# Mixture-of-experts layers: the third block of rows transposed whole, and the transposes of the next expert split in two pairs

## The chip, the cores and the metric

The kernel runs on one core of a Trainium2 chip. The metric is the time that one execution takes on the device, in microseconds (us), as the median of several runs.

## The reference, cut to what matters

The input x has 8 x 1024 rows of 512 float32 numbers. Three layers follow each other: a mixture-of-experts layer, an attention layer with 16 heads, and the same mixture-of-experts layer again. Each works on the layer-normed x and is added to x, the experts' layers with a factor of 0.5. The change lies in the experts' layers alone:

```python
xt = x.reshape(T, H)                       # T = 8192 rows, H = 512
logits = xt @ w_router                     # E = 32 experts
top1 = argmax(softmax(logits)); gate = probs[top1]
pos = position of the row among those of its expert
accepted = pos < C                         # C = 320 = 1.25 * T / E
buf[e, pos] = xt                           # (E, C, H), the accepted rows by expert
g = einsum("ech,ehf->ecf", buf, w_gate)
u = einsum("ech,ehf->ecf", buf, w_up)
y = einsum("ecf,efh->ech", silu(g) * u, w_down)
out = xt + where(accepted, y[slot] * gate, 0)
```

Everything is float32.

## The kernel before

**Experts one after another.** After routing, `experts` sorts the 32 experts by how many rows they got and takes one of several compiled profiles of widths. In the profiled execution the widths are 320 for the first 10 experts in either layer, then 288 for 9, 256 for 8 and 224 for 5. A width of over 256 means three blocks of up to 128 rows (`NB` = 3; the third block has 64 rows of an expert's capacity of 320), a width of up to 256 means two. `gather` fetches the rows of an expert two experts ahead, by indirect DMAs of POOL's queue. `load` orders the three weight matrices wg, wu and wd of the next expert on SP's queue; they have two buffers each, so each load waits until the last matmul that read the buffer is done.

**One expert.** `feed(now, following, after)` runs one expert (`now`) and prepares the next (`following`). The engines PE, ACT, DVE and POOL work in the order that the code writes down; nothing is reordered. Its steps:

1. DVE takes the statistics of the following expert's rows (`measure`).
2. For each of four parts f of the hidden width, `gated` (line 705) multiplies the transposed rows bT with wg and wu into the PSUM tiles gp and up; ACT takes the silu of gp into sg, and DVE multiplies sg and up into a (line 729). After f = 0 ACT normalizes the following rows into b (line 172), after f = 1 DVE prepares their residuals (line 186).
3. `put_others` (line 646, 650) scales and writes two blocks of other rows, those that pass an expert layer by.
4. `transpose` (lines 685 to 696) turns the following expert's b, four column blocks k of 128, each over all its blocks of rows, into a PSUM tile of tag tp (two buffers), which DVE copies to bT (line 696).
5. The down products: for each block i of rows PE sums four products with wd into yp (line 744; line 752 for the third block, which is laid out as 2 x 64 rows of 256), DVE scales yp by the gate and adds the residual into ys (line 748, 758), and POOL writes ys to its rows by an indirect DMA (line 762).

A float32 matmul on 512 columns appears in the trace as two records, so a block of down products has eight, while a transpose has one.

**The transposes before the change.** In `transpose` a block of the expert that has fewer than 128 rows within the capacity of 320 is turned at its own size:

```python
for i, at in enumerate(range(0, C, P)):
    m = min(P, C - at)
    nc.tensor.transpose(
        tp[:, at : at + m], to.b[:m, i, k * P : (k + 1) * P], s.ident[:m, :m]
    )
```

So the third block is a transpose of 64 rows (in the trace "64*128" for its weight load, with b as the weights, and 64 moving columns of the identity). `begin` does the same once per layer for the first expert, with four PSUM tiles at once (line 608).

PSUM has two buffers for each of the tags tp, gp, up and yp.

Of the kernel before, what the change touches and what calls it, by code (L numbers as in the profile page):

```python
# [13 lines left out]
F32 = mybir.dt.float32  # L14
# [8 lines left out]
P = 128  # L23
# [12 lines left out]
def at_once(steps):  # L36

    while True:
        try:
            next(steps)  # L40
        except StopIteration as end:
            return end.value
# [503 lines left out]
class Expert:  # L546
# [34 lines left out]
    def begin(self, to):  # L581

        nc, s, ap = self.nc, self.s, self.ap
        to.mv = ap.tile([P, to.NB, 2], F32, tag="mv", name="mv")
        to.by = [
            ap.tile([P, to.NB], F32, tag=name, name=name) for name in ("rstd", "nmr", "r2", "n2")
        ]
        to.b = ap.tile([P, s.NB, s.D], F32, tag="b", name="b")
        to.bT = ap.tile([P, s.KD, s.C], F32, tag="bT", name="bT")
        steps = []  # L590
        for i in range(to.NB):
            at = slice(i, i + 1)
            s.stats(ap, to.mv[:, i, :], to.x[:, i, :])
            steps.append(s.normalizing(ap, to.mv[:, at, :], [t[:, at] for t in to.by]))
            next(steps[i])
            if i:
                at_once(steps[i - 1])
        at_once(steps[-1])
        assert s.KD == 4
        tps = [  # L600
            self.ps.tile([P, s.C], F32, tag=tag, name="tp") for tag in ("tp", "up", "tp", "up")
        ]
        C = min(to.NB * P, s.C)
        for i in range(to.NB):
            s.normalize(to.b[:, i, :], to.x[:, i, :], to.by, i)
            m = min(P, C - i * P)
            for k, tp in enumerate(tps):
                nc.tensor.transpose(
                    tp[:, i * P : i * P + m], to.b[:m, i, k * P : (k + 1) * P],
                    s.ident[:m, :m],  # L610
                )
        for k, tp in enumerate(tps):
            (nc.scalar.copy if k % 2 else nc.vector.tensor_copy)(to.bT[:, k, 0:C], tp[:, 0:C])  # L613
        self.rests(to)
# [67 lines left out]
                    s.NB - 1, p,  # L682
                )

    def transpose(self, to):
        nc, s = self.nc, self.s
        C = min(to.NB * P, s.C)
        to.bT = self.ap.tile([P, s.KD, s.C], F32, tag="bT", name="bT")
        for k in range(s.KD):
            tp = self.ps.tile([P, C], F32, tag="tp", name="tp")  # L690
            for i, at in enumerate(range(0, C, P)):
                m = min(P, C - at)
                nc.tensor.transpose(  # L693
                    tp[:, at : at + m], to.b[:m, i, k * P : (k + 1) * P], s.ident[:m, :m]
                )
            nc.vector.tensor_copy(to.bT[:, k, 0:C], tp)

    def gated(self, to, f):
        nc, s, width = self.nc, self.s, to.width
# [13 lines left out]
    def feed(self, now, following, after):  # L713

        nc, s = self.nc, self.s
        n, half, KF = s.last, s.D // 2, s.KF
        a, wd = s.acts[now.r % 2], now.weights[2]
        others = self.fetch_others(now.r) if self.others else None  # L720
        if following:
            self.measure(following)
        later = after and after()
        for f in range(KF):
            sg, up = self.gated(now, f)
            if following and f == 0:
                self.scales(following)
                self.normalize(following)
            nc.vector.tensor_tensor(a[:, f, 0 : now.width], sg, up, ALU.mult)  # L729
            if following and f == 1:  # L730
                self.rests(following)
        if others:
            self.put_others(now.r, others)
        if following:
            self.transpose(following)
        for i in range(now.NB):
            yp = self.ps.tile([P, s.D], F32, tag="yp", name="yp")
            ys = self.ap.tile([P, s.D], F32, tag="ys", bufs=3, name="ys")
            gate = self.gates[:, i * s.E + now.r : i * s.E + now.r + 1]
            index = self.go[:, i * s.E + now.r : i * s.E + now.r + 1]  # L740
            to = self.views[now.r * s.NB + i]
            if i < s.NB - 1:
                for f in range(KF):
                    nc.tensor.matmul(  # L744
                        yp, a[:, f, i * P : (i + 1) * P], wd[:, f, :],
                        start=(f == 0), stop=(f == KF - 1),
                    )
                nc.vector.scalar_tensor_tensor(ys, yp, gate, now.x[:, i, :], ALU.mult, ALU.add)  # L748
            else:
                for f in range(KF):  # L750
                    for c in range(2):
                        nc.tensor.matmul(  # L752
                            yp[c * n : (c + 1) * n, 0:half], a[:, f, i * P : s.C],
                            wd[:, f, c * half : (c + 1) * half],
                            start=(f == 0), stop=(f == KF - 1),
                        )
                ys = ys[:, 0:half]
                nc.vector.scalar_tensor_tensor(
                    ys, yp[:, 0:half], gate, now.rest, ALU.mult, ALU.add
                )  # L760
                to = to.rearrange("t (c d) -> (t c) d", c=2)
            nc.gpsimd.indirect_dma_start(
                out=to, out_offset=bass.IndirectOffsetOnAxis(ap=index, axis=0),
                in_=ys, in_offset=None, bounds_check=to.shape[0] - 1, oob_is_err=False,
            )
        return later


class Attention:
# [95 lines left out]
    def stage(self, top, sum_, fill, begin, whole=False):  # L865

        for i in range(self.SLOTS):  # L870
            self.now += 1
            prs = {}
            first, second = self.phases(top, sum_)
            self.phase(i, *first, prs)
            for rank, task in begin.get(i, ()):
                self.start(task, rank)
            self.step(1.3 if top else 4)
            if self.half:
                assert i not in fill
                self.group()  # L880
            elif i in fill:
                self.half = fill[i]()
                self.group()
                if whole:
                    self.group()
            if second:
                self.phase(i, *second, prs)
            self.last_sums()
            if sum_:
                self.behind.append((*sum_, i, prs))  # L890
            if not self.half:
                self.product()
            self.step(0.9)
# [603 lines left out]
```

## Time and profile before

| what | us |
|---|---|
| median of 3 runs | 4915.01 |
| lowest and highest | 4911.32, 4916.07 |
| the profiled execution | 4901.53 |
| its span in the profile | 4899.7 |
| PE (TensorE) busy in it | 4644.6 |
| transposes at line 693 | 640, of them 144 with 64 rows |

The profile is of one execution. Its page gives the busy time by engine, the chain of work that ended last and the costliest groups of instructions; "PE" is a matmul, "PEld" the load of its weights, which can overlap matmuls before it. A row of a group reads: line, engine, operation, out<-in by the tiles' names, shapes, count, then busy us, mean ns of one, and the idle time of the engine before it with what ended that idle time. A row of the timeline reads: start us, us, engine, line, operation, and the count of merged instructions. The expert stages run from about 172 to 989 us and from about 4078 us to the end of the span.

### The profile page before, as it was taken

How to read it: one execution, taken by the hardware profiler on the slowest of the kernel's cores; microseconds unless marked ns; L12 is line 12 of the kernel's file. 1: busy time of each engine (PE TensorE's matmuls, PEld its weight loads, DVE VectorE, ACT ScalarE, POOL GpSimd, SP SyncE). 2: the span in 40 equal slices, each digit the busy share in tenths (PEclk: the TensorE clock that was granted, in tenths of full speed). 3: DMA queues.
4: the chain of work that ended last, by engine and by line, in shares of the span. 5: the costliest groups of instructions: out<-in, count | busy, mean ns of one | idle time of the engine just before them, and what ended most of it. 6: DMA issues, size and time to landing. Idle time of an engine off the chain costs nothing.

```text
span 4899.7 us, 68858 instructions
## 1 busy us (share of the span) xinstructions
PE 4644.6 (95%) x24572; PEld 2131.3 (43%) x24572; DVE 2848.9 (58%) x5568; ACT 2924.6 (60%) x5856; POOL 790.6 (16%) x787
## 2 busy tenths in 40 slices
PE   6799999968899999999999999999999877999998
PEld 4466667722233333333333333333333224666676
DVE  8433333346666767767767767777777733333332
ACT  6211111118998888888888888888888831111111
POOL 4423332210000010110110100100001002222221
PEclk8899999979999999999999999999999988999999
DMA  4455556531112212212212212212211124445554
GB/s 140 164 169 184 183 192 204 183 92 29 32 31 59 74 38 64 69 42 65 69 41 68 72 38 67 70 40 66 63 46 54 51 68 166 161 155 174 165 183 135
DMA packets 290580, 486.01 MB, mean 99 GB/s; under 512 B 47895, under 2 KB 83169, under 8 KB 290224
## 3 DMA queue, kind: packets, MB, share of 16 engines
q1 hardware_dynamic: 255376, 404.36, 26.4%
q0 software_dynamic: 34560, 76.93, 5.1%
q8 instruction: 196, 3.21, 0.3%
q14 instruction: 160, 1.31, 0.1%
q10 hardware_dynamic: 288, 0.20, 0.0%
HBM read 380.11 MB, written 89.72 MB: 96 GB/s over the span
## 4 chain that ended last, share of the span: by engine, by line
PE 82%; DVE 8%; ACT 4%; issue 3%; DMA 2%; POOL 1%; SPq 1%; DVEq 0%; POOLq 0%; ACTq 0%
PE sa L1219 13%; PE gp L705 10%; PE up L705 9%; PE pq L1124 9%; PE po L1301 9%; PE yp L744 9%; PE sb L1199 6%; PE px L1327 4%; PE pv L1169 4%; PE sb L1226 3%; ACT junk L1238 2%; DVE nm L1234 2%; PE tp L693 2%; PE tp L194 1%; PE yp L752 1%
## 5 line engine op out<-in xcount | busy, mean ns | idle before, releaser
L1234 DVE TENSOR_REDUCE nm<-sa 128x2 f32<-128x1024 f32 x1024 | 1249.3, 1221 | 648.8 <-PE sa L1219 386.5
L1238 ACT ACTIVATE junk<-sa,nm 128x512 f32<-128x512 f32 x2048 | 1408.2, 688 | 257.7 <-DVE nm L1234 178.6
L1219 PE MATMUL sa<-k,q 32*128 32x512 f32 x4096 | 1149.0, 644 | 17.9 <-ACT junk L1238 11.2
L1231 ACT ACTIVATE pr<-sb 128x1024 f32<-128x1024 f32 x1024 | 1041.3, 1018 | 99.4 <-PE sb L1226 95.9
L1226 PE MATMUL sb<-q,k 32*128 32x512 f32 x4096 | 1062.0, 602 | 0.0
L710 ACT ACTIVATE sg<-gp 128x320 f32<-128x320 f32 (+3 forms) x256 | 102.8, 402 | 1231.6 <-PE gp L705 1081.8
L1149 POOL TENSOR_TENSOR raw<-raw,a 128x512 f32<-128x512 f32 x128 | 164.4, 1284 | 2401.3 <-DMA rot<-raw 1694.1
L1301 PE MATMUL po<-pr,v 128*32 128x512 f32 x4096 | 548.0, 606 | 0.1
L705 PE MATMUL gp<-bT,wg 128*128 128x320 f32 (+3 forms) x2048 | 532.4, 403 | 0.5 <-DVE bT L613 0.5
L705 PE MATMUL up<-bT,wu 128*128 128x320 f32 (+3 forms) x2048 | 525.0, 399 | 0.0
L1124 PE MATMUL pq<-hT,wqk 128*128 128x512 f32 x1024 | 512.2, 624 | 5.4 <-DVE raw L1139 4.4
L744 PE MATMUL yp<-wd,a 128*128 128x512 f32 x1024 | 453.7, 596 | 0.0
L705 PEld LDWEIGHTS gp<-bT,wg 128*128 128x128 f32 x2048 | 387.5, 191 | 116.4 <-issue 28.1
L1199 PE MATMUL sb<-mrow,ones 3*128 3x512 bf16 x2048 | 392.7, 384 | 41.8 <-ACT pr L1231 40.5
L705 PEld LDWEIGHTS up<-bT,wu 128*128 128x128 f32 x2048 | 389.2, 190 | 94.4 <-issue 0.4
L729 DVE TENSOR_TENSOR a<-sg,up 128x320 f32<-128x320 f32 (+3 forms) x256 | 114.1, 446 | 543.3 <-PE up L705 512.8
L1199 PEld LDWEIGHTS <-ones 3*128 3x128 bf16 x2048 | 99.7, 91 | 708.6 <-issue 670.7
L1238 ACT ACTIVATION_READ_ACCUMULATOR junk<-sa,nm 128x1 f32 x2048 | 398.1, 194 | 0.0
L1226 PEld LDWEIGHTS sb<-q,k 32*128 32x128 f32 x4096 | 359.5, 184 | 0.1
L1219 PEld LDWEIGHTS sa<-k,q 32*128 32x128 f32 x4096 | 304.8, 183 | 81.5 <-ACT pr L1231 30.1
L1124 PEld LDWEIGHTS pq<-hT,wqk 128*128 128x128 f32 x1024 | 176.5, 191 | 324.8 <-issue 228.0
L748 DVE SCALAR_TENSOR_TENSOR ys<-yp,gates,x 128x512 f32<-128x512 f32 x128 | 96.2, 751 | 368.9 <-PE yp L744 368.9
(178 smaller groups left out, 4277.3 us busy)
## 6 DMA issues: line engine op xcount, KB each, us to landing
wg<-in_w_gate SPq DMA_DIRECT2D x64, 1024.0 KB
wu<-in_w_up SPq DMA_DIRECT2D x64, 1024.0 KB
wd<-in_w_down SPq DMA_DIRECT2D x64, 1024.0 KB
rot<-raw SPq DMA_DIRECT2D x1024, 32.0 KB
all<-in_x SPq DMA_DIRECT2D x32, 512.0 KB
xt<-first_rows SPq DMA_DIRECT2D x64, 256.0 KB
xr<-first_rows SPq DMA_DIRECT2D x64, 256.0 KB
d<-inverse SPq DMA_DIRECT2D x256, 64.0 KB
```

What stands on the lines that cost most here:

```text
L705: nc.tensor.matmul(acc, w[:, k, f * P : (f + 1) * P], to.bT[:, k, 0:width], start=(k == 0), stop=(k == s.KD - 1),)
L744: nc.tensor.matmul(yp, a[:, f, i * P : (i + 1) * P], wd[:, f, :], start=(f == 0), stop=(f == KF - 1),)
L1124: nc.tensor.matmul(acc, w[:, which, k, :], self.hT[b, n][:, k, :], start=(k == 0), stop=(k == KD - 1),)
L1169: nc.tensor.matmul(acc, hT[:, k, at : at + P], self.w_vo[:, k, :], start=(k == 0), stop=(k == KD - 1),)
L1199: nc.tensor.matmul(sb[:, h, :], self.ones16[at : at + 3, :], row[at : at + 3, :], start=True, stop=False,)
L1219: nc.tensor.matmul(sa[:, h, :], qa[at, (g * 4 + j) * P : (g * 4 + j + 1) * P], ka[at, m * 512 : (m + 1) * 512], start=True, stop=True,)
L1226: nc.tensor.matmul(sb[:, h, :], k[at, t * P : (t + 1) * P], q[at, n * 512 : (n + 1) * 512], start=False, stop=True,)
L1231: nc.scalar.activation(pr, sb, AF.Exp)
L1234: nc.vector.tensor_reduce(nm[:, m, j, pair : pair + 2], sa, AX.X, ALU.max, negate=True)
L1238: nc.scalar.activation(self.junk, sa[:, h - pair, :], AF.Exp, bias=nm[:, m, j, h : h + 1], accum_out=se[:, m, j, h : h + 1],)
L1301: nc.tensor.matmul(self.po[at : at + HD, :], self.v[b][t][:, c * P + at : c * P + at + HD], prs[h // 2 * 2][:, h % 2, :], start=(t == 0), ...
L1327: nc.tensor.matmul(acc, self.oT[b, c, half][:, j * P : (j + 1) * P], self.w_vo[:, c, :], start=False, stop=(c == KD - 1),)
```

## The change

The third block is transposed at its full 128 rows and 128 columns, in `begin` and in `transpose`; the PSUM tiles tp are made 384 columns wide for three blocks, and only the first 320 columns are copied on, as before. The rows behind the 64 used ones are in b anyway, since gathering and normalizing treat 128 rows of each block.

`transpose` now takes the column blocks that it is to do. The first two (k = 0, 1) stand ahead of the first block's down products, the other two (k = 2, 3) ahead of the second block's. On DVE the copies of the second pair thereby stand behind the first block's ys. The order and the DMAs of ACT, POOL and SP stay as they were.

Of the semaphores that PE waits for, these move: the third and the fourth down product of a block wait for DVE's a of f = 2 and f = 3, and the first gp products of the next expert at k = 2 and k = 3 wait for DVE's copies.

```diff
@@ begin
         tps = [
-            self.ps.tile([P, s.C], F32, tag=tag, name="tp") for tag in ("tp", "up", "tp", "up")
+            self.ps.tile([P, s.NB * P], F32, tag=tag, name="tp") for tag in ("tp", "up", "tp", "up")
         ]
         C = min(to.NB * P, s.C)
         for i in range(to.NB):
             s.normalize(to.b[:, i, :], to.x[:, i, :], to.by, i)
-            m = min(P, C - i * P)
             for k, tp in enumerate(tps):
                 nc.tensor.transpose(
-                    tp[:, i * P : i * P + m], to.b[:m, i, k * P : (k + 1) * P],
-                    s.ident[:m, :m],
+                    tp[:, i * P : (i + 1) * P], to.b[:, i, k * P : (k + 1) * P], s.ident
                 )
@@ transpose
-    def transpose(self, to):
+    def transpose(self, to, ks):
         nc, s = self.nc, self.s
         C = min(to.NB * P, s.C)
-        to.bT = self.ap.tile([P, s.KD, s.C], F32, tag="bT", name="bT")
-        for k in range(s.KD):
-            tp = self.ps.tile([P, C], F32, tag="tp", name="tp")
-            for i, at in enumerate(range(0, C, P)):
-                m = min(P, C - at)
+        if 0 in ks:
+            to.bT = self.ap.tile([P, s.KD, s.C], F32, tag="bT", name="bT")
+        for k in ks:
+            tp = self.ps.tile([P, to.NB * P], F32, tag="tp", name="tp")
+            for i in range(to.NB):
                 nc.tensor.transpose(
-                    tp[:, at : at + m], to.b[:m, i, k * P : (k + 1) * P], s.ident[:m, :m]
+                    tp[:, i * P : (i + 1) * P], to.b[:, i, k * P : (k + 1) * P], s.ident
                 )
-            nc.vector.tensor_copy(to.bT[:, k, 0:C], tp)
+            nc.vector.tensor_copy(to.bT[:, k, 0:C], tp[:, 0:C])
@@ feed
         if others:
             self.put_others(now.r, others)
-        if following:
-            self.transpose(following)
         for i in range(now.NB):
+            if following and i < 2:
+                self.transpose(following, range(i * s.KD // 2, (i + 1) * s.KD // 2))
             yp = self.ps.tile([P, s.D], F32, tag="yp", name="yp")
```

## Prediction

> **What bounds the kernel now.** I read the page first, then the busy time by stretch of an expert stage, then the groups of line 693 (the transposes that the change touches), and last the order of time around single transposes. The page says who carries the span:
>
> ```profile
> span 4899.7 us, 68858 instructions
> PE 4644.6 (95%) x24572; PEld 2131.3 (43%) x24572; DVE 2848.9 (58%) x5568; ACT 2924.6 (60%) x5856; POOL 790.6 (16%) x787
> PE 82%; DVE 8%; ACT 4%; issue 3%; DMA 2%; POOL 1%; SPq 1%; DVEq 0%; POOLq 0%; ACTq 0%
> ```
>
> PE (TensorE) is busy 95% of the span and holds 82% of the chain that ended last. The expert stages, asked by stretch (columns: stretch, length, then busy time and count of PE, weight loads, DVE, ACT, POOL; granted clock; DMA share; GB/s), are tighter still:
>
> ```profile
> 450.00:690.00 240.00, 239.75 (x964) 155.87 (x963) 88.83 (x220) 45.81 (x80) 76.99 (x79) 1.00 0.57 186
> 690.00:960.00 270.00, 263.85 (x1101) 197.16 (x1100) 91.72 (x246) 54.32 (x99) 80.46 (x85) 1.00 0.62 206
> ```
>
> PE is busy for 239.75 of 240 us with DVE at 37% and DMA at 57%, clock at 1.00. So whatever PE time is removed here shortens the stage, unless something with slack becomes late. But busy is not the same as full: matmuls overlap, and a badly spaced one is still counted busy. The groups of the transposes (busy us, mean ns | idle before), for the first expert stage, show this:
>
> ```profile
> L693 PE MATMUL tp<-ident,b 128*128 128x128 f32 x248 | 48.3, 290 | 6.9 <-DVE bT L696 6.2
> L693 PE MATMUL tp<-ident,b 64*128 64x64 f32 x72 | 19.7, 274 | 0.0
> ```
>
> The small transposes (64 rows) occupy 19.7/72 = 0.274 us each, their whole duration: nothing overlaps them. The whole ones take 48.3/248 = 0.195. Now one phase of each kind, PE only, then the weight loads of the first:
>
> ```profile
> 640.78 0.41 PE L705 MATMUL up<-bT,wu 128*128 128x288 f32 x1
> 641.02 2.40 PE L693 MATMUL tp<-ident,b 128*128 128x128 f32 x12
> 643.35 0.70 PE L744 MATMUL yp<-wd,a 128*128 128x512 f32 x1
> ```
>
> ```profile
> 641.33 0.40 PEld L693 LDWEIGHTS tp<-ident,b 64*128 64x128 f32 x3 [0.17 <-issue]
> 641.90 0.14 PEld L693 LDWEIGHTS tp<-ident,b 64*128 64x128 f32 x1 [0.17 <-issue]
> 642.20 0.20 PEld L693 LDWEIGHTS tp<-ident,b 128*128 128x128 f32 x2 [0.16 <-DVE bT L696]
> ```
>
> ```profile
> 741.22 0.59 PE L705 MATMUL up<-bT,wu 128*128 128x256 f32 x2
> 741.65 0.60 PE L693 MATMUL tp<-ident,b 128*128 128x128 f32 x4
> 742.74 0.77 PE L693 MATMUL tp<-ident,b 128*128 128x128 f32 x4 [0.48 <-DVE bT L696]
> 743.34 1.02 PE L744 MATMUL yp<-wd,a 128*128 128x512 f32 x2
> ```
>
> The phase with three blocks lasts 643.35 - 641.02 = 2.33 us for 12 transposes. The one with two blocks lasts 743.34 - 741.65 = 1.69 us for 8, of which four come in a row: 0.60 us from first start to last end, less one duration of 0.273, over three steps: 0.109 us apart. That is the cadence without hindrance. The starts of the single records give the rest. With three blocks they lie 0.109, 0.203, 0.203, 0.165, 0.203 and so on apart: 0.20 into and out of every 64-row transpose, 0.165 for the next after it, since its weight load is no longer ahead (the 0.17 us idle before the 64-row loads). And once a phase there is a wait for DVE: with two PSUM buffers of tag tp, the third transpose tile waits until DVE has copied out the first; with three blocks that step takes 0.30 to 0.33 us, with two blocks 0.72 to 0.79, followed by three steps of 0.165.
>
> **The change part by part.**
>
> *How much there is to win.* The trace's groups have 640 transposes at L693, 144 of 64 rows: 144/4 = 36 phases of three blocks, and (640 - 432)/8 = 26 of two. From start of a phase to the first yp, the trace has 20 phases of 2.360 us (expert at work 320 wide), 16 of 2.328 (288), 2 of 1.721, 16 of 1.686 (256), 8 of 1.654 (224): 128.1 us in all.
>
> *What it becomes.* The count of transposes stays, all are 128x128, and no 64-row load is left, so each step is 0.109 us, the step into yp too (743.23 to 743.34). 36 x 12 x 0.1093 + 26 x 8 x 0.1093 = 70.0 us. Saved: **58.1 us**: 33.1 from whole third blocks (36 phases; 2.345 mean less 0.113 of stall less 1.312), 25.0 from the stall (36 x 0.113 + 26 x 0.805).
>
> *A rule that speaks against the first edit.* Row: 64-row transposes cost 0.203 us a step, whole ones 0.109. The Trainium skill, "TensorE: Matmul & The Clock Gate", section "Back-to-back issue gap", lists the gap by free size: 134 cycles for 128 columns, about 60 up to 64, so widening 64 to 128 more than doubles it. By that rule (estimate from 0.109) a small transpose should take 0.049 and the edit would lose 144 x 0.060 = 8.6 us. The trace decides, as its 0.203 was measured in this very stream. The tiling page of the skill ("TensorEngine Tiling (Array Packing)", "Key Properties") names what fits: a change of tiling mode drains the engine. That it is the change of 64 to 128 rows, not the change of PSUM tile, is seen in the two-block phase, whose four in a row go from the first tile to the second at 0.109.
>
> *Transposes in two pairs.* The third and fourth tile now come after the first block's down products (8 records of yp 0.429 us apart, 3.43 us). DVE copies the first two tiles right after the product for a at f=3: in the phase at 641.02 that product ends at +0.73, two copies at 0.48 follow by +1.75. PE comes back for tile three at 0.65 + 3.43 = +4.09: the wait is gone with 2.3 us to spare. The semaphore itself stays on the loads of tiles three and four, already satisfied; the trace has no satisfied DVE wait there. Ends: 0, as for the satisfied wait for wd at the first yp (0.109 after the last transpose), and 0.056 (0.165 less 0.109) for each, 62 x 2 x 0.056 = 7 us; a gain is excluded, 0.109 being the floor. I take 0, the nearer row. A new wait: yp for f=2 and f=3 now waits for DVE's a, which the transposes used to cover. f=2 comes at +0.65 + 4 x 0.429 = +2.37 (two blocks: +2.15), a is ready at +0.73: cost nothing, cover 1.4 us; without it, up to that much per expert.
>
> *DVE.* The last two copies now stand behind the first ys in DVE's queue, which waits for yp. In a two-block phase yp's last record starts at 0.44 + 3.00; ys starts 0.63 after that, as now (922.44 against 921.81), takes 0.75, so it ends at +4.8, and two copies at 0.41 are done by +5.7. The next gp needs the third of its operands at 0.44 + 3.43 + 0.44 + 3.43 + 4 x 0.19 = +8.5, the earliest (224 wide). Cost nothing, cover 2.8 us. ys(1), behind the copies, waits for PE until +8.0. With three blocks another 1.86 us of yp lies between.
>
> *Queues.* ACT, POOL and SP keep order and DMAs; the first ys, and its write on POOL, comes 1.2 to 1.7 us earlier, behind the two writes of other rows (done by +2.3, POOL idle 4 us after them). ACT loses one wait. PSUM tiles grow from 320 to 384 columns, copies keep their sizes: nothing.
>
> *begin().* Once per layer, at half clock: four 64-row transposes become whole. A step is 0.213 there and 0.107 for the small, but the step into the small ones, now 0.35, becomes 0.213. +0.13 us for the last, about -0.13 for the first; between -0.2 and +0.3 us per layer. I take 0.
>
> *Sum.* 4899.7 - 58.1 = 4841.6 us of span, 4843.4 for the profiled execution (4901.53). That execution is 13.5 us below the median of the shown runs and outside their 4911 to 4916, so I take the difference, not the level: 4915.0 - 58.1 = **4857 us**.
>
> **The rivals.**
>
> *A: turning between products and transposes costs.* Two more turns per phase. If each cost what a turn between 64 and 128 rows does (0.094 + 0.056), 62 x 2 x 0.15 = 18.6 us come back: 4876. For: such turns exist on this engine. Against: up to tp takes up's own cadence (640.78 to 641.02), tp to yp 0.109.
>
> *B: it does not do what it says for the third block;* the 0.203 has another cause and stays. Then only the stall goes: 25 us, 4890. Against: no 64-row load remains, and 109 ns rows are all around.
>
> *C: slower, through wd.* yp of the next expert now comes sooner after wd is ordered at the end of the last one. In the narrowest experts wd is issued at 925.87 and the next yp starts at 939.42; by the DMA share, the rush is over at 934:
>
> ```profile
> 930.00:934.00 4.00, 4.00 (x23) 4.00 (x23) 1.32 (x4) 1.66 (x4) 1.51 (x2) 1.00 0.77 272
> 934.00:936.00 2.00, 2.00 (x12) 2.00 (x11) 0.39 (x1) 0.00 (x0) 0.00 (x0) 1.00 0.16 66
> ```
>
> So 8.1 us are used of 13.55, and 12.3 remain (1.65 - 0.44 less). Beyond 12.3 each us costs one in each of the 26 two-block phases; all 58 us are gone when wd takes 58/26 = 2.2 us more, 14.6, and beyond that it is slower: at 15.5 us 26 x 3.2 = 83 us are lost, 4857 + 83 = 4940. For: DMA moves 206 GB/s here and the same bytes come in less time. Against: four free us.
>
> **How the numbers follow.** 0.2% of 4915, 9.8 us, is about what a measurement of this kernel can tell from no change. The full gain has 0.86 (4843 to 4872: 50 to 62 us, and the level of a run, which moved 13 us between the profiled one and the median); A and B together 0.08, all faster; no change 0.03; C 0.03. Faster 0.94, same 0.03, slower 0.03. The range 4842 to 4874 holds the first case and a part of A.
>
> **What would show it.** Right: no 64-row group at the transposes; groups of six (three blocks) or four transposes 0.109 apart, twice per expert with yp between; no idle of PE before tp left by DVE's bT; a period of 27.5 to 27.6 us for 320-wide experts (28.63 now) and 19.85 for 224-wide (20.63). A: steps over 0.109 at the ends of the groups. B: 0.2 within them. C: PE idle before yp, released by the DMA of wd. I am wrong if gp is seen waiting for DVE's bT, or if PE's saving is there and the span did not follow.

## The result, and the profile after

The changed kernel takes 4849.66 us (median of 4 runs, 4847.76 to 4851.12) against 4914.85 us before (4911.32 to 4916.07, a fourth run included): 65.2 us less, a ratio of 0.9868 with a 95% interval of 0.9851 to 0.9885. The prediction was 4857 us within 4842 to 4874, so 58 us less.

The lines of the page that answer to those shown of before:

```profile
span 4847.2 us, 68820 instructions
PE 4596.5 (95%) x24572; PEld 2128.0 (44%) x24572; DVE 2836.3 (59%) x5568; ACT 2923.5 (60%) x5856; POOL 790.4 (16%) x787
```

PE issues the same 24572 matmuls and is busy for 48.1 us less; no other engine's busy time moves by more than 13 us. The expert stage by stretch (columns as before):

```profile
450.00:690.00 240.00, 240.00 (x1001) 161.12 (x1000) 89.26 (x227) 47.60 (x83) 79.74 (x82) 1.00 0.60 194
690.00:950.00 260.00, 260.00 (x1100) 197.51 (x1099) 90.04 (x243) 52.83 (x97) 80.32 (x85) 1.00 0.63 210
```

In the same 240 us of the clock PE now fits 1001 matmuls where it had 964 (it is further on in the experts, so part of this is narrower work), at the same granted clock of 1.00; in the narrower experts its last 6 us of idle time are gone. The groups of the transposes, of the whole execution (now line 692, and 607 for the first expert):

```profile
L692 PE MATMUL tp<-ident,b 128*128 128x128 f32 x640 | 90.1, 273 | 0.0
L607 PE MATMUL tp<-ident,b 128*128 128x128 f32 x24 | 6.2, 430 | 17.3 <-ACT b L172 17.3
```

There is one form left, 90.1/640 = 0.141 us each in overlap, and the idle time in front of it is 0.0. A phase of three blocks in order of time, PE and then DVE:

```profile
632.56 0.82 PE L692 MATMUL tp<-ident,b 128*128 128x128 f32 x6
633.22 1.02 PE L745 MATMUL yp<-wd,a 128*128 128x512 f32 x2
...
636.65 0.82 PE L692 MATMUL tp<-ident,b 128*128 128x128 f32 x6
637.31 1.02 PE L745 MATMUL yp<-wd,a 128*128 128x512 f32 x2
```

```profile
632.83 0.45 DVE L728 TENSOR_TENSOR a<-sg,up 128x288 f32<-128x288 f32 x1 [3.43 <-PE tp L692]
633.20 0.88 DVE L695 COPY bT<-tp 128x320 f32<-128x320 f32 x2
636.85 0.75 DVE L749 SCALAR_TENSOR_TENSOR ys<-yp,gates,x 128x512 f32<-128x512 f32 x1 [2.77 <-PE yp L745]
637.52 0.88 DVE L695 COPY bT<-tp 128x320 f32<-128x320 f32 x2
```

Each group of six lasts 0.82 us to its last end, less one duration of 0.273, over five steps: 0.109. The first yp follows 0.655 after the start of the group. DVE's first two copies are done at 634.08, 2.6 us before PE comes back for the third tile; the second two, behind ys, at 638.40.

**Where the time came from.** I summed the steps between starts of consecutive PE records in the two expert stages, from the first gp to the last yp. The stages lasted 810.12 and 809.05 us and now last 777.96 and 777.58: 63.6 us less. Of these, the phases of transposes fell from 128.1 to 69.9 us (58.2); the steps of yp fell by 3.5; those of gp and up by 1.9, which belong to the clock and not to the change (see below). So the change itself is worth 61.7 us by its steps. The interval of the ratio, some 57 to 73 us, holds this as well as the 65.2 of the medians. The stage between (3093.5) and the tail (11.7) stayed equal to 0.1 us.

The span of the profiled executions fell by only 52.5 us, because the stage ahead of the first expert took 186.4 us in this one and 175.4 in the one of before. An experiment below shows the same difference without the change.

### The profile page after: what moved, and what is told of

Same layout as the page of the kernel before. It is cut to its first block, busy times and chain, and to the rows that moved or that the text cites. A ratio compares the mean times of both kernels' runs of the same rounds, so it can differ in the third digit from the quotient of the medians.

```text
span 4847.2 us, 68820 instructions
## 1 busy us (share of the span) xinstructions
PE 4596.5 (95%) x24572; PEld 2128.0 (44%) x24572; DVE 2836.3 (59%) x5568; ACT 2923.5 (60%) x5856; POOL 790.4 (16%) x787
## 4 chain that ended last, share of the span: by engine, by line
PE 82%; DVE 7%; ACT 4%; issue 3%; DMA 2%; POOL 1%; SPq 1%; another core or an unknown queue 0%; DVEq 0%; POOLq 0%; ACTq 0%
PE sa L1220 13%; PE gp L704 10%; PE up L704 9%; PE pq L1125 9%; PE po L1302 9%; PE yp L745 9%; PE sb L1200 6%; PE px L1328 4%; PE pv L1170 4%; PE sb L1227 3%; ACT junk L1239 2%; DVE nm L1235 2%; PE tp L194 2%; DMA table<-row,slot 1%; PE yp L753 1%
## 5 line engine op out<-in xcount | busy, mean ns | idle before, releaser
L1220 PE MATMUL sa<-k,q 32*128 32x512 f32 x4096 | 1149.1, 645 | 17.9 <-ACT junk L1239 11.1
```

The source lines that it names most:

```text
L1220: nc.tensor.matmul(sa[:, h, :], qa[at, (g * 4 + j) * P : (g * 4 + j + 1) * P], ka[at, m * 512 : (m + 1) * 512], start=True, stop=True,)
```

## The experiments

**e3, the kernel before again,** without an edit, for a second profile.

> The kernel before unchanged, for a second profile: the profiled execution of before was 13.5 us below the median of its runs, and the stage ahead of the first expert took 175.4 us in it, 186.4 in the profile of the changed kernel. Theory: that stage varies from run to run with the landing of the routing table's scattered writes (20.4 and 27.1 us at its end), so a second profile of before may show up to 186 us there, with the expert stages at 810 and 809 us as in the first. Rival: the change itself made that stage 11 us longer; then it is 175 us here again, in an execution of about 4901 us.

Measured: one execution at 4914.9 us, the first gp at 186.97 us, expert stages of 809.7 and 809.7 us. The chain of waits of the first profile of before, and of this one, in the routing stage (start, length, what):

```profile
146.55 20.42 DMA table<-row,slot
```

```profile
151.40 27.20 DMA table<-row,slot
```

The same kernel shows both landing times of the routing table's writes. With the changed kernel's two profiles (27.14 and 20.14 us) they come in both kernels: the 11 us do not belong to the change, and the expert stages do not depend on them. Of the 11.6 us between these two profiles of before, the landing makes 6.8; the other 4.8 lie ahead of it, where the last writes start later (151.40 for 146.55). What the level goes with stays open. On record, it goes along with the chip: e1 to e4 ran on one chip, where the first gp comes at 185.7 to 187.0 us and the unchanged kernel took 4912 to 4918; e5 and e6 ran on another, with 175.1 and 175.5 us, and 4901 to 4905. The chips of the first two profiles are not on record.

**e1, whole third blocks alone,** the four tiles together as before.

```diff
+        if following:
+            self.transpose(following, range(s.KD))
         for i in range(now.NB):
-            if following and i < 2:
-                self.transpose(following, range(i * s.KD // 2, (i + 1) * s.KD // 2))
```

> One part of the change alone: the third block is transposed whole, but all four tiles stay together ahead of the first down products. Theory (the two parts need each other): the third tile then still waits for DVE's copy of the first, which DVE can only start with the product for a at f=3, so it starts where it did (1.18 to 1.22 us into the phase), and the fourth 0.57 us later behind the second copy; then three steps (0.165, 0.109, 0.109) into yp. A phase of three blocks comes to 2.13 to 2.16 us for 2.33 to 2.36 before, and the first yp step falls from 0.533 to 0.432 us: 36 x 0.30 = 11 us less than before, phases of two blocks as before. Rival (my prediction's split): whole third blocks are worth 33 us by themselves, the phase 1.4 us long.

Measured: 4893.22 us against 4913.07, ratio 0.9957 (0.9940 to 0.9974). The expert stages are 19.5 us shorter, of which 13.1 come from the phases, 3.7 from yp steps and 2.7 from gp and up steps at the first expert (see the clock below). A phase of three blocks, PE:

```profile
615.76 0.82 PE L692 MATMUL tp<-ident,b 128*128 128x128 f32 x6
616.94 0.94 PE L692 MATMUL tp<-ident,b 128*128 128x128 f32 x6 [0.36 <-DVE bT L695]
617.72 0.59 PE L743 MATMUL yp<-wd,a 128*128 128x512 f32 x1
```

The first six transposes finish early, and then PE stands still: the third tile starts 616.94 - 615.76 = 1.18 us into the phase, the very place it had before (642.20 - 641.02). The step in front of it, between starts, grew from 0.30 to 0.64 us. So whole blocks do not earn what they save; most of it turns into the wait for DVE's copy. The phase is 1.96 to 2.00 us, 0.36 shorter, where I expected 0.2: the fourth tile came 0.40 us after the third and not 0.57, since the second copy now follows the first directly. The medians differ by 19.9 us, with an interval of 13 to 29: more than the 11 us expected, but the rival, 33 us from this part alone, is refuted.

**e2, the two pairs alone,** with the third block of 64 rows in the phases.

```diff
             for i in range(to.NB):
+                m = min(P, C - i * P)
                 nc.tensor.transpose(
-                    tp[:, i * P : (i + 1) * P], to.b[:, i, k * P : (k + 1) * P], s.ident
+                    tp[:, i * P : i * P + m], to.b[:m, i, k * P : (k + 1) * P],
+                    s.ident[:m, :m],
                 )
```

> The other part alone: two pairs, with the third block at 64 rows in the phases. Theory: phases of two blocks become 2 x 0.437 us as in the full change (26 x 0.81 = 21 us), those of three blocks 2 x 1.09 us for 2.345, but the slow first yp step of 0.533 now comes twice, so they gain 2.345 + 0.102 - 2.18 - 0.204 = 0.07 us each, 2 us: 23 us less than before in all. Rival (my prediction's split): 25 us. Rival 2: if the slow step belonged to the wait for DVE and not to 64 rows, all steps here are 0.109 and it is as fast as the full change, 64 us less than before.

Measured: 4884.49 us, ratio 0.9939 (0.9922 to 0.9956, or 22 to 38 us less); the expert stages 24.3 us shorter, of which 27.3 from the phases, minus 3.8 in yp steps, and 0.8 from gp and up. The times cannot tell the 23 us of the theory from the 25 of the prediction's split; the steps (27.26 less 3.82, so 23.4) are those of the theory. A pair of tiles with three blocks, and its groups of transposes:

```profile
572.71 1.15 PE L693 MATMUL tp<-ident,b 128*128 128x128 f32 x6
573.79 1.55 PE L747 MATMUL yp<-wd,a 128*128 128x512 f32 x3
```

```profile
L693 PE MATMUL tp<-ident,b 128*128 128x128 f32 x496 | 90.2, 281 | 0.0
L693 PE MATMUL tp<-ident,b 64*128 64x64 f32 x144 | 39.2, 272 | 0.0
```

The idle time is 0.0, so the wait for DVE is gone. The pair still lasts 573.79 - 572.71 = 1.08 us to the first yp, and its single steps are 0.109, 0.203, 0.202, 0.165, 0.203, 0.202 as in the kernel before. So the slow steps are not an effect of the wait, and rival 2 is refuted. Nor are they one of narrower PSUM tiles, which are 384 columns wide here too. The first yp step is slow (0.533 us for 0.432) after each of the 72 pairs that end in a small transpose, which is what the yp steps lost.

**e4, the small ones next to each other,** in two pairs.

```diff
-        for k in ks:
-            tp = self.ps.tile([P, to.NB * P], F32, tag="tp", name="tp")
-            for i in range(to.NB):
+        tps = {k: self.ps.tile([P, to.NB * P], F32, tag="tp", name="tp") for k in ks}
+        for blocks in (range(min(to.NB, 2)), range(2, to.NB)):
+            for k in ks:
+                for i in blocks:
+                    m = min(P, C - i * P)
...
```

> Two pairs, third block at 64 rows, but within a pair the whole transposes of both tiles come first and then the two of 64 rows next to each other. Theory (the price is paid at each change between 128 and 64 rows): one entry at 0.203, then 0.055 to 0.11 from one 64-row transpose to the next, one exit at 0.205 with the first yp step at 0.533: a pair lasts 0.79 to 0.84 us for 1.09 with the small ones apart, 72 x 0.25 to 0.30 = 18 to 21 us faster than that kernel, some 42 us faster than before. Rival (each small transpose is slow by itself): 0.203 between the two small ones as well, a pair of 0.94 us, 11 us faster than that kernel.

Measured: 4867.12 us, ratio 0.9906 (0.9890 to 0.9923), 17.4 us less than e2; the phases are 20.7 us shorter than there (18 to 21 expected; the profiled execution of e2 was 4.9 us above its median). A pair of tiles, and the groups:

```profile
587.90 0.87 PE L693 MATMUL tp<-ident,b 128*128 128x128 f32 x6
588.70 3.70 PE L748 MATMUL yp<-wd,a 128*128 128x512 f32 x8
```

```profile
L693 PE MATMUL tp<-ident,b 128*128 128x128 f32 x496 | 74.4, 273 | 0.0
L693 PE MATMUL tp<-ident,b 64*128 64x64 f32 x144 | 24.3, 249 | 0.0
```

The busy time of the small ones falls from 39.2 to 24.3 us, but this is not yet a proof: a group's busy time leaves out only what its own members overlap, so a small one among whole ones always shows its full 0.272. The steps decide. They are 0.109 three times, 0.203 into the first small one, 0.115 from small to small, 0.152 from the second small one to yp, then 0.533 for the first yp step: a pair of 588.70 - 587.90 = 0.80 us. The rival's 0.203 between two small ones is refuted: the price is paid at the change between 128 and 64 rows. A change in the moving columns alone has no such price: the step from up, 288 columns, into the transposes is 0.242 us like those within up, and from a whole transpose into yp, 512 columns, it is 0.109. And a small transpose next to its like still needs 0.115 us, no less than a whole one: its half width earns nothing in this stream.

**e5, the third block folded,** on top of the full change. The gathered third block holds its 64 rows twice, so both halves of the partitions can carry half the columns, and one transpose serves two column blocks.

```diff
@@ normalize, for the third block
...
+            for c in range(2):
+                p = slice(c * n, (c + 1) * n)
+                self.nc.scalar.activation(
+                    to.b[p, i, 0:half], to.x[p, i, c * half : (c + 1) * half], AF.Identity,
+                    bias=to.by[1][p, i : i + 1], scale=to.by[0][p, i : i + 1],
+                )
@@ transpose, with W = 2 * P, and wide for the third block at k < 2
...
+            if wide:
+                nc.tensor.transpose(
+                    tp[:, W : W + P], to.b[:, 2, k * P : (k + 1) * P], s.ident
+                )
+            to_ = C if wide else W
+            nc.vector.tensor_copy(to.bT[:, k, 0:to_], tp[:, 0:to_])
+            if wide:
+                nc.vector.tensor_copy(to.bT[:, k + 2, W:C], tp[:, C : W + P])
```

> The full change, and the third block folded: its 64 rows stand twice in the gathered rows (128 partitions), so ACT normalizes columns 0 to 255 on the first 64 partitions and columns 256 to 511 on the others, and one whole transpose then serves the column blocks k and k+2. The first pair of tiles has six transposes, the second four; DVE makes two more copies of 64 columns in the first pair, behind the others in slack. Theory (PE's steps of 0.109 us are all that counts in these phases): 36 x 2 x 0.109 = 7.8 us less than the full change, about 4842 us where the full change has 4850. Rival: the two more copies and the two narrower normalizing operations make bT or b late, a wait of PE for them shows and the gain is gone, 4850 or more.

**e6, the changed kernel again,** beside e5 on the same chip.

> The changed kernel itself once more, on the same chip as the folded one, as its measure. Theory: 0.987 of before and expert stages of 777 to 779 us each, the differences of 1 to 2 us between profiles being the half clock at the first expert, which lasts 2 to 5 us[...]. Rival: the 65 us of the first comparison were partly another level of the runs; then 58 us, 0.988, and the stages differ from 778 us.

Measured: e6 4838.01 us (4836.25 to 4839.62) against 4902.24 for before, 64.2 less, ratio 0.9867 (0.9852 to 0.9882); expert stages 778.5 and 778.2 us. So the saving repeats at another level of the runs. The rival, 58 us and stages that differ from 778, falls by the stages; by the times alone 58 us lie at the edge of the interval. e5: 4828.49 us (4827.48 to 4828.81), ratio to before 0.9848 (0.9834 to 0.9861), 9.5 us less than e6. Its groups (two lines of the code now):

```profile
L702 PE MATMUL tp<-ident,b 128*128 128x128 f32 x496 | 78.3, 273 | 0.0
L706 PE MATMUL tp<-ident,b 128*128 128x128 f32 x72 | 19.6, 273 | 0.0
```

568 transposes where there were 640, none waits, and the expert stages together are 8.0 us shorter than in e6, 7.8 having been expected. The profiled executions also differ by 2.3 us in the stage between, with the attention layer, which the edit does not touch and which took 3090.5 to 3095.2 us in the eight profiles; so the 1.5 us by which the medians differ more are not counted for the edit. DVE's and ACT's added operations cost PE nothing: the profile shows no wait of PE in its expert stages. It is the fastest of the kernels here.

## Why the prediction was right, and where not

- **PE bounds the expert stages, and what is removed there shortens them:** right. 63.6 us left the stages, and what lies between and behind them kept its length to 0.1 us.
- **The phases:** right. 58.1 us forecast, 58.2 measured; every step 0.109, and no satisfied wait cost anything (of the 7 us allowed for the two loads that keep a semaphore of DVE, none came).
- **The first yp step:** missed, 3.5 us. I counted a phase up to the start of the first yp and took its own step for granted. After a 64-row transpose that step was 0.533 us instead of 0.432, in 36 phases. The two views of yp (min, median, max in ns), before and after, show it in the maximum:

```profile
L744 PE MATMUL yp<-wd,a x1024: 592/592/697, 197.4 to 4888.0; 128*128 128x512 f32 x171
```

```profile
L745 PE MATMUL yp<-wd,a x1024: 592/592/596, 205.4 to 4835.4; 128*128 128x512 f32 x171
```

- **begin() taken as nothing:** the stages began at half clock in both kernels, and how long that lasted differed: 4.9 and 2.6 us after the first gp of the two layers before, 2.1 and 1.4 after. A gp step of 320 columns takes 0.53 us there and 0.27 after it, so half of the 4.0 us of difference is lost: 2.0, about the 1.9 us found in gp and up. In e3 it was 3.8 and 4.0, in e1 0.3 and 1.7, so it comes and goes with the run, and that it added to the gain here is luck:

```profile
175.30:180.20 4.90, 4.85 (x9) 3.20 (x10) 3.89 (x9) 1.83 (x4) 1.99 (x3) 0.50 0.64 169
```

```profile
186.00:188.50 2.50, 2.50 (x7) 1.56 (x6) 2.48 (x6) 2.13 (x3) 1.60 (x3) 0.50 0.46 120
188.50:192.00 3.50, 3.50 (x14) 2.42 (x13) 2.20 (x6) 0.44 (x1) 0.59 (x2) 0.99 0.74 237
```

(The first row is of before, the others of after; the granted clock is the third number from the end.)

- **The split of the gain, 33.1 us for whole blocks and 25.0 for the stall:** wrong for the first. Without the clock's share, e1 gives 16.7 us (13.07 in the phases, 3.65 at the first yp steps) and e2 23.4; together they give 61.7, so 21.6 us come only when both are done. Of these, 17.9 lie in the phases. The failed step took the stall as a fixed length (0.113 us) that could be set aside. It is a fixed end: DVE sets when the third tile may start, and what is saved ahead of it is waited off. The other 3.7 come from the first yp step, which the pairs alone make slow twice per phase. So whole blocks are worth 16.7 us before the pairs and 38.3 after them. The sum came out right because it was taken from the phases as a whole, before and after, and the split did not enter it.
- **The change of rows, not the width:** right. A small transpose cost 0.203 next to whole ones (e2), and 0.115 even beside its like (e4), against 0.109 for a whole one; the 0.049 that the prediction worked out as the rule against it is seen nowhere at full clock. That rule did not fit the case: the section of the Trainium skill that has the table ("TensorE: Matmul & The Clock Gate", "Back-to-back issue gap") gives it for the gap of an isolated matmul, and says that in a stream of loads and matmuls both set the spacing; here each of the 640 transposes has its own load. That the price is a drain of the engine, as the tiling page has it, no run shows; the runs show where it is paid.
- **A reading that was wrong without harm:** the small transposes were said to overlap with nothing, since their busy time was their whole duration. The whole one behind each starts 0.203 us after it, within its 0.273; the busy time of their group cannot show that. The sum used the steps.
- **The covers:** right. DVE's copies behind ys end at 638.40 in the phase shown, 5.84 us into it; a (+0.72) is there long before f = 2 of yp. The profile shows no wait of PE in either expert stage. The period of an expert is 27.48 us (320 wide, 27.5 to 27.6 forecast) and 19.85 (224 wide, as forecast); the first lies just under its range, since the first yp step lost 0.10 us as well.
- **The rivals:** A (turns within yp cost) is refuted by steps of 0.429 into and 0.109 out of the second pair; B by e2 and the groups; C by the absence of any wait of PE for wd.
- **The level:** forecasting the difference from the median, not from the profiled execution's own time, was right; of the 13.4 us between the spans of e3 and of the first profile of before, 11.6 lie ahead of the first gp.

## What to carry to other kernels

Ask of each stall whether it is a length or a date: if another engine sets when it ends, what is saved ahead of it is lost until the stall itself goes, and two edits can be worth more together than apart. On PE, count steps between starts, into the first instruction of what follows, and not busy time: a stage busy for 239.75 of 240 us still held most of the gain here. Keep neighbouring matmuls at the same number of rows; in this stream of transposes a partly filled block was cheaper whole, and cheaper still when its empty half was given other work.

## What was not expected of the hardware

- A change from 128 to 64 rows and back costs 0.094 us at each side of the small transpose, 0.056 at the step after it if a whole transpose follows, and 0.10 us in the next step if a float32 product follows. Between two small transposes there is no such cost (0.115 us a step), and the exit to yp is then 0.152 instead of 0.203.
- The down products of the third block, 128 rows by 64 columns, pay much the same, before and after the change. In the kernel before, behind the phase at 641.02:

```profile
643.35 7.13 PE L744 MATMUL yp<-wd,a 128*128 128x512 f32 x16
650.41 1.95 PE L752 MATMUL yp<-wd,a 128*64 128x256 f32 x16
652.29 2.21 PE L705 MATMUL gp<-bT,wg 128*128 128x288 f32 x8
```

The step into them is 0.523 us where 0.429 is plain, the next between pairs of them 0.260 for 0.209, the step out 0.309, and the first gp step 0.347 for 0.243. Over 38 such blocks this makes some 13 us, an estimate from these steps. So the price is not one of transposes, nor of rows alone. No run tried to remove it.
- At half clock, in begin(), the later ones of four small transposes in a row ran 0.107 us apart and whole ones 0.213; at full clock small and whole ones both stand near 0.11. Only the whole ones followed the clock.
- The last writes of the routing table took 20.1 to 20.4 us to land in three of these profiles and 27.1 to 27.4 in four (in that of e2 the chain holds 23.3), at the end of the stage that moves the level of a run by 11 us.
